# A four-layer graph network on one core: another order of the first loads, and batch norms worked out block by block

## The chip, the core and the metric

The kernel runs on one core of one Trainium2 chip. The metric is the device time of one execution in microseconds (us); a median stands for several executions. A profile is one of these executions, with every instruction's start and length.  Each group of experiments went to one chip, whose number came with the results: 15, 11 and 13.

Engines in the profile: PE is TensorE (PEld its weight loads), DVE is VectorE, ACT is ScalarE, POOL is GpSimd, SP is SyncE; SPq, ACTq and POOLq are their issues of DMA transfers. A line number such as L339 is a line of the kernel named. The change moves lines: L320 of the kernel before is L339 of the changed one (first matmul of layer 1's second product, "the first second-layer matmul" below), L266 is L285 (py), L762 is L775, L834 is L842 to L845.

Names in the profile lines: in layer 0, pt and xt are transposes of x and their copies; pq the query and value products; zs the gathered rows and es the attention scores made of them; adc the row copies of a quad's attention matrix; py its product with the values, yt the copy of that, po the product that follows. In layer 3, ag is the aggregate, ph (from ag) the first half's product and po (from z or zl) the second half's.

## The reference, cut to what matters

x is 128 batches of 128 nodes with 256 features. Four layers follow each other; after each, the input is added and a layer norm taken.

```python
# layer 0: attention over 512 edges
e = einsum(leaky_relu(Xq[:, src] + Xq[:, dst]), a) + log(adj[src, dst] + 1e-8)
attn = segment_softmax(e, src);  Y[src] += attn * Xv[:, dst];  return Y @ W_out.T
# layer 1: h = relu(S @ (x @ W1)); h = relu(S @ (h @ W2)); S @ (h @ W3), with S = adj * adj
# layer 2: three products with the diagonal, upper and lower part of adj, plus a bias
# layer 3: two batch norms, each over all 128 * 128 rows
h = relu(batchnorm(agg @ W1.T + b1, g1, be1))
out = batchnorm(h @ W2.T + b2, g2, be2)
```

Each batch norm needs sums over the whole batch: everything before it must be finished before anything after it starts.

## The kernel before

Batches go in 32 quads of four. Layers 0, 1, 2 and the first half of layer 3 run as one software pipeline, an iteration per quad. `start()` fills this pipeline: it sorts the edges, takes the first quads through attention and loads the weights in between. Then the second half of layer 3 runs over all quads, and an output part normalizes, adds and stores. The parts that matter here:

```python
# start(), cut
    xg1 = load_x(1, "xg", 2)
    ... wo, w1 loaded;  zeros stored to att_dram[0]
    values_in(0, xg0, nc.scalar.copy);  values(0, 0..3)       # TensorE; q stored to DRAM
    ... edges sorted on TensorE;  gather(0) on GpSimd
    nc.scalar.activation(weight, weight, AF.Ln)
    values_in(1, xg1, nc.scalar.copy);  values(1, 0..3)
    ... xg3, w2, xr0 loaded;  zeros stored to att_dram[1]      # 3.5 MB with w1
    for c in range(NE):
        score(0, c)                                            # VectorE, needs gathered rows
    gather(1, ...)
    ... softmax of quad 0;  attention(0);  scatter(0)          # 4 GpSimd scatters, then a 1 MB load
    ... w3, l2w, bias, l3w1 loaded
    gather(2);  score(1, 0..2)
    for j in range(QB):
        by_row(0, j)                                           # ScalarE: row copies of the load
    stage_a(0)                                                 # py, yt, po
    values_in(3, xg3);  values(3, 0..3);  ...
    attention(1);  scatter(1)                                  # before the loop
# hidden(k, c): layer 3's first half, block c
    nc.scalar.copy(s.zt[:, c, :], ph)
    nc.vector.bn_stats(st1[:, c, k, :], ph)
# after the loop: b1, g1, be1, w2t, b2, g2, be2 are loaded through GpSimd, then
    sc1, sh1 = batch_norm(st1, K3, b1, g1, be1, "n1")          # all four blocks at once
    ... second half of layer 3 over all quads, then
    sc2, sh2 = batch_norm(st2, DC, b2, g2, be2, "n2")
# apply(q), the output of a quad: four multiplications on ScalarE, one store by GpSimd
```

## Time and profile before

| | |
|---|---|
| timed executions | 3437.02, 3444.74, 3446.68 us |
| profiled execution | 3427.55 us, span 3425.8 us |
| TensorE busy | 97% of the span |
| first second-layer matmul | 128.65 us |
| one quad in the loop | 93.21 us |
| stop before layer 3's second half | 11.28 us |
| one quad in that half, in the output part | 6.866, 3.06 us |

The page shows the span in 40 slices; each digit is the busy share of a slice in tenths:

```profile
PE   5899999999999999999999999999999999989987
DMA  7512333333323222333333323222333331024447
```

TensorE is full except in the first slices, around slice 36 and at the end. A gain of some microseconds can only come from there. The profiled execution is faster than every timed one, by 9 us or more.

### The profile page before, as it was taken

What the parts mean: (1) busy time and instruction counts of PE and PEld (TensorE: products, weight loads), DVE (VectorE), ACT (ScalarE), POOL (GpSimd) and SP (SyncE); (2) the same over time, 40 slices, a digit from 0 to 9 for tenths busy, and PEclk for the clock granted to TensorE, in tenths of its full rate; (3) what the DMA queues carried; (4) which work ended last, traced back from release to release, by engine and by line L of the source; (5) the groups of instructions that cost most, each with busy time, mean ns of one, the idle gap of its engine ahead of it and who ended that gap; (6) DMA issues with size and microseconds to landing.
All of it is one profiled execution on the core that took longest, in us unless ns stands there. A gap on an engine that the chain in (4) does not pass through costs nothing.

```text
span 3425.8 us, 34423 instructions
## 1 busy us (share of the span) xinstructions
PE 3326.6 (97%) x13328; PEld 2111.0 (62%) x13328; DVE 1715.3 (50%) x3367; ACT 1016.9 (30%) x1751; POOL 641.9 (19%) x535
## 2 busy tenths in 40 slices
PE   5899999999999999999999999999999999989987
PEld 2566666666666666666666666666666666654444
DVE  6545555444554544555445554554555444223358
ACT  2222222222222222222222222222222222225438
POOL 4211222222211111222122221111122220000015
PEclk8899999999999999999999999999999999999999
DMA  7512333333323222333333323222333331024447
GB/s 227 159 46 87 96 99 99 99 87 99 99 80 99 82 74 80 93 99 99 99 87 99 99 81 98 87 77 72 92 99 99 99 93 38 19 88 152 153 156 250
DMA packets 117316, 346.01 MB, mean 101 GB/s; under 512 B 12832, under 2 KB 50080, under 8 KB 108832
## 3 DMA queue, kind: packets, MB, share of 16 engines
q0 software_dynamic: 46032, 152.61, 18.0%
q1 hardware_dynamic: 69344, 189.48, 15.4%
q8 instruction: 106, 1.74, 0.2%
q10 hardware_dynamic: 1776, 1.71, 0.2%
q14 instruction: 58, 0.48, 0.0%
HBM read 257.77 MB, written 85.98 MB: 100 GB/s over the span
## 4 chain that ended last, share of the span: by engine, by line
PE 94%; ACT 2%; DVE 2%; DMA 1%; issue 0%; POOL 0%; ACTq 0%; POOLq 0%; DVEq 0%
PE ph L320 26%; PE p L333 13%; PE po L381 10%; PE po L762 6%; PE ph L421 6%; PE pq L170 6%; PE ph L300 6%; PE po L275 3%; PE pm L310 3%; PE pm L367 3%; PE py L266 2%; PE po L344 2%; PE pm L286 2%; PE pa L406 2%; ACT x3l L833 1%; PE pt L372 1%
## 5 line engine op out<-in xcount | busy, mean ns | idle before, releaser
L320 PE MATMUL ph<-m,w 128*128 128x512 f32 x2048 | 884.2, 592 | 0.0
L320 PEld LDWEIGHTS ph<-m,w 128*128 128x128 f32 x2048 | 389.0, 190 | 476.1 <-issue 474.5
L186 POOL DMA_INDIRECT zs<-qd,src_idx x124 | 147.6, 1191 | 1715.7 <-DMA qd<-qt 1678.5
L333 PE MATMUL p<-w,h 128*128 128x256 f32 x2048 | 450.5, 381 | 0.0
L333 PEld LDWEIGHTS p<-w,h 128*128 128x128 f32 x2048 | 386.6, 190 | 53.0 <-issue 1.0
L381 PE MATMUL po<-l2w,ms 128*128 128x256 f32 x1536 | 347.5, 379 | 1.3 <-DVE ms L373 1.3
L323 ACT ACTIVATE h<-ph 128x512 f32<-128x512 f32 x256 | 152.8, 597 | 585.3 <-PE ph L320 585.2
L381 PEld LDWEIGHTS po<-l2w,ms 128*128 128x128 f32 x1536 | 284.3, 190 | 36.2 <-DVE ms L373 1.6
L170 PE MATMUL pq<-wqv,xt 128*128 128x512 f32 x512 | 232.9, 608 | 7.8 <-DVE xt L158 4.0
L300 PE MATMUL ph<-w,mx 128*128 128x512 f32 x512 | 235.8, 593 | 0.0
L421 PE MATMUL ph<-ag,l3w 128*128 128x512 f32 x512 | 225.4, 593 | 0.8 <-ACT ag L410 0.8
L186 POOL DMA_INDIRECT zs<-qd,dst_idx x124 | 195.1, 1574 | 139.8 <-DMA zs<-qd,src_idx 123.4
L762 PE MATMUL po<-zl,l3w 128*128 128x512 f32 x496 | 213.0, 592 | 0.0
L346 DVE TENSOR_TENSOR xr<-xr,po 128x512 f32<-128x512 f32 x64 | 43.8, 684 | 334.9 <-PE po L344 334.9
L242 POOL DMA_INDIRECT attd<-at,att_idx x128 | 127.5, 996 | 425.9 <-DMA attd<-at,att_idx 285.3
L158 DVE COPY xt<-pt 128x512 f32<-128x512 f32 x58 | 37.4, 686 | 279.9 <-PE pt L156 279.9
L421 PEld LDWEIGHTS ph<-ag,l3w 128*128 128x128 f32 x512 | 96.9, 190 | 122.1 <-issue 112.6
L92 ACT ACTIVATE ln_sd<-ln_mv,eps 128x2 f32<-128x2 f32 x192 | 56.5, 294 | 388.2 <-DVE ln_mv L87 388.2
L170 PEld LDWEIGHTS pq<-wqv,xt 128*128 128x128 f32 x512 | 97.2, 195 | 119.9 <-issue 110.5
L762 PEld LDWEIGHTS po<-zl,l3w 128*128 128x128 f32 x496 | 94.2, 190 | 118.6 <-issue 115.0
L100 DVE TENSOR_SCALAR xr<-xr,ln_mv,ln_rs 128x256 f32<-128x256 f32 x384 | 162.9, 466 | 6.9
L310 PEld LDWEIGHTS pm<-wt_t,h 128*128 128x128 f32 x1024 | 131.8, 191 | 47.7 <-issue 39.9
(201 smaller groups left out, 4112.6 us busy)
## 6 DMA issues: line engine op xcount, KB each, us to landing
ad<-attd SPq DMA_DIRECT2D x32, 1024.0 KB, 4.8
zd<-z SPq DMA_DIRECT2D x31, 1024.0 KB, 7.9
zl<-zd SPq DMA_DIRECT2D x62, 512.0 KB, 4.2
xg<-in_x_dram SPq DMA_DIRECT2D x32, 512.0 KB, 4.3
xr<-in_x_dram SPq DMA_DIRECT2D x32, 512.0 KB, 5.8
x3d<-xr SPq DMA_DIRECT2D x32, 512.0 KB, 2.9
x3l<-x3d SPq DMA_DIRECT2D x32, 512.0 KB, 4.3
out_dram<-x3l POOLq DMA_DIRECT2D x32, 512.0 KB, 4.6
```

The source lines that it names most:

```text
L100: nc.vector.tensor_scalar(r[:, i, :], r[:, i, :], mv[:, i, 0:1], rs[:, i:i + 1], op0=ALU.subtract, op1=ALU.mult)
L170: nc.tensor.matmul(pq, s.xts[i // 2][:, i % 2, c, :], wqv[:, c, :], start=(c == 0), stop=(c == DC - 1))
L186: nc.gpsimd.indirect_dma_start(out=s.z[c], out_offset=None, in_=s.qd, in_offset=bass.IndirectOffsetOnAxis(ap=idx[:, c:c + 1], axis=0), com ...
L242: nc.gpsimd.indirect_dma_start(out=ad, out_offset=bass.IndirectOffsetOnAxis(ap=att_idx[:, c:c + 1], axis=0), in_=s.at[:, c, :], in_offset= ...
L300: nc.tensor.matmul(ph, s.mx[i // 2 * 2][:, i % 2, dc, :], w1_sb[:, dc, :], start=(dc == 0), stop=(dc == DC - 1))
L310: nc.tensor.matmul(pm[:, c, :], s.h1[i][:, c * P:(c + 1) * P], wt_t, start=True, stop=True)
L320: nc.tensor.matmul(ph, w2_sb[:, c, f * P:(f + 1) * P], s.m2[:, c].rearrange("p b n -> p (b n)"), start=(c == 0), stop=(c == K1 - 1))
L323: nc.scalar.activation(h.rearrange("p b n -> p (b n)"), ph, AF.Relu)
L333: nc.tensor.matmul(p3[:, t * D:(t + 1) * D], s.h2[f][:, j + t, :], w3_sb[:, f, :], start=(f == 0), stop=(f == K2 - 1))
L381: nc.tensor.matmul(po[:, i % 2, :], mss[i][:, t, dc, :], l2w[:, t, dc, :], start=(n3 == 0), stop=(n3 == 3 * DC - 1))
L421: nc.tensor.matmul(ph, l3w1[:, dc, c * P:(c + 1) * P], s.ag[:, dc, :], start=(dc == 0), stop=(dc == DC - 1))
L762: nc.tensor.matmul(po, w2t[:, c, o * P:(o + 1) * P], z[c // 2][:, c % 2, :], start=(c == 0), stop=(c == K3 - 1))
```

## The change

Intent: let nothing that is needed late compete with the first quad's attention; have the parameters of layer 3 on the chip before they are needed; let TensorE go on with a block of layer 3 as soon as that block's statistics are known; shorten the end. The core of the diff:

```diff
@@ start(): loads @@
             xg1 = load_x(1, "xg", 2)
+            nc.sync.dma_start(att_dram[0][...], zero)
             nc.sync.dma_start(wo, ...)
-            nc.sync.dma_start(w1_sb, ...)
-            nc.sync.dma_start(att_dram[0][...], zero)
@@ start(): quad 1 straight behind src_row, ahead of the logarithm @@
+            values_in(1, xg1, nc.scalar.copy)
+            for i in range(QB):
+                values(1, i, nc.scalar.copy, nc.scalar)
+            gather(1, [...])
...
             nc.scalar.activation(weight, weight, AF.Ln)
-            values_in(1, xg1, nc.scalar.copy)   # and values(1, ..), gather(1) further below
...
             xg3 = load_x(3, "xg", 2)
-            nc.sync.dma_start(w2_sb, ...)
             quads[0].xr = load_x(0, "xr", 3, wk)
-            nc.sync.dma_start(att_dram[1][...], zero)
...
             scatter(0)
+            nc.sync.dma_start(w1_sb, ...)
+            nc.sync.dma_start(w2_sb, ...)
+            nc.sync.dma_start(att_dram[1][...], zero)
...
+            nc.sync.dma_start(w2t, ...)          # and the six vectors of layer 3
             for j in range(QB):
-                by_row(0, j)
+                by_row(0, j, nc.vector.tensor_copy if j % 2 else None)
             stage_a(0)
-            values_in(3, xg3)
+            values_in(3, xg3, nc.scalar.copy)
...
-            attention(1)
-            scatter(1)
@@ iteration(): in the first one @@
                     second(c, f)
+                    if first_one and f == 0:
+                        attention(b)
+                        scatter(b)
@@ hidden(k, c) @@
+            if k < NQ - 1:
+                nc.scalar.copy(s.zt[:, c, :], ph)
             nc.vector.bn_stats(st1[:, c, k, :], ph)
             if k == NQ - 1:
+                batch_norm(st1, c, bn1, sc1, sh1, c)
+                nc.scalar.activation(s.zt[:, c, :], ph, AF.Relu, bias=sh1[...], scale=sc1[...])
@@ second half of layer 3: last quad first, its matmuls block by block; after the last quad's stats @@
+                    if q == order[-1]:
+                        batch_norm(st2, o, bn2, sc2, sh2, K3 + o)
+                        halves(0, o, outs[0])
+                        spread(o)
                     nc.vector.tensor_copy(ag[:, o, :], po[o])
@@ apply(): the last quad @@
+                    if q == NQ - 1 and i < 2:
+                        nc.vector.tensor_scalar(x3s[q][:, i, :], src_, mvs[q][:, i, 0:1], rs[:, i:i + 1], ...)
+                if q == NQ - 1:
+                    nc.sync.dma_start(o_q[:, :2], x3s[q][:, :2, :])
+                    nc.scalar.dma_start(o_q[:, 2:], x3s[q][:, 2:, :])
```

Some small buffers share space to make room for w2t and the vectors (the zeros take m2's buffer, three adjacency tiles one scratch buffer).

## The prediction

> **What bounds the kernel now.** I read the table by stage first (busy time of each engine in stretches of the span), then the chain that ended last, then TensorE's own timeline. From the table (columns: stretch, busy us and instruction count of each engine, granted TensorE clock, DMA share, GB/s):
>
> ```profile
> 0.00:30.00 30.00, 20.99 (x75) 11.48 (x76) 16.43 (x50) 8.07 (x16) 14.30 (x18) 0.97 0.74 236
> 30.00:60.00 30.00, 14.79 (x61) 9.24 (x61) 18.60 (x20) 4.62 (x11) 11.15 (x9) 0.74 0.96 284
> 60.00:90.00 30.00, 9.36 (x40) 4.77 (x40) 16.95 (x26) 7.37 (x15) 15.03 (x14) 0.71 0.69 184
> ...
> 1000.00:1100.00 100.00, 100.00 (x444) 66.47 (x444) 50.75 (x99) 28.23 (x47) 21.37 (x18) 1.00 0.36 105
> ...
> 3050.00:3080.00 30.00, 19.44 (x81) 13.59 (x80) 14.01 (x33) 4.99 (x10) 5.42 (x8) 0.94 0.52 176
> ```
>
> In the loop TensorE is busy 100 us of 100, so nothing the change does there can pay. It is idle in the first 129 us, around 3075 and near the end. The same places in TensorE's timeline (start, length, operation, in brackets the idle time before it and its releaser):
>
> ```profile
> 55.76 1.02 PE L208 MATMUL pe<-ident,es 128*16 128x128 f32 x4 [15.21 <-DVE es L201]
> ...
> 88.72 3.99 PE L266 MATMUL py<-adc,xv 128*64 128x128 f32 x32 [16.85 <-ACT adc L252]
> ...
> 101.53 9.82 PE L170 MATMUL pq<-wqv,xt 128*128 128x512 f32 x16 [3.98 <-DVE xt L158]
> ```
>
> Two holes of 15.21 and 16.85 us hang on the first quad's attention. What lies behind them, from the chain (start, length, piece):
>
> ```profile
> 41.00 10.51 DMA qd<-qt
> ...
> 67.64 7.89 DMA attd<-at,att_idx
> 75.53 0.27 issue
> 75.81 2.14 DMA attd<-at,att_idx
> ...
> 82.71 4.88 DMA ad<-attd
> ...
> 3076.80 6.06 DMA be<-in_l_be_dram
> 3082.89 221.92 PE po L762 x512
> ```
>
> Quad 1's store takes 10.51 us because 2 MB of w2, 0.5 MB of x and 1 MB of zeros were issued at 37 to 39 us. That holds up quad 1's gather on GpSimd, and the scatter of quad 0's attention stands behind that gather. The last two lines show the batch norm waiting for parameters fetched only after layer 3's first half: TensorE stops for 11.28 us (3071.6 to 3082.9). From 3082.9 to 3304.8 TensorE is full; then it waits 5.38 us for the second batch norm. The output part runs at 3.06 us a quad with ScalarE full (20.00 us of 20 between 3360 and 3380).
>
> **What the Trainium skill says.** "DMA: Bandwidth & Descriptors", section "Issuing engines are not separate DMA queues": transfers of all issuing engines run on the same 16 DMA engines and interleave. The trace agrees: the DMA share is 0.96 between 30 and 60 us, and the store issued by ScalarE is slow because of loads issued by SyncE. "TensorE: Matmul & The Clock Gate", "What's actually happening": after a window of idling the array runs at half clock for about 3.4 us. Here, after the 11.28 us stop, weight loads come 0.86 us apart until 3087.05 and 0.43 us afterwards, so a stop costs about 2 us on top of itself. "ScalarE: Activation LUTs", "What ACT_TABLE_LOAD costs": 1283 ns plus a drain; the trace has 1.28 us. I need this for the moved logarithm.
>
> **Part 1, first loads (all times us; ~ marks my estimates).** w1, w2 and the second zero transfer (3.5 MB) move behind the load of quad 0's attention matrix. Quad 1's values are no longer interrupted: before, ScalarE sat on the logarithm until 27.5 and held xt. Now its copies run after src_row at 23.9, TensorE starts at ~24.5, 16 records of 0.43 end at ~31.4, and the store is issued at ~31.8 instead of 41.0. The price: the logarithm comes after these copies. Table load ~32.2 to 33.5, then 0.2, then four VectorE operations of 0.2, so VectorE stands idle from 27.4 to ~33.8 and the keep/reset rows (2.13) end at ~36.6. So the first score starts at ~36.6, not 33.23. But before, the third and fourth scores waited 4.72 and 1.84 for gathered rows; now, with four scores of 3.78 back to back and 0.45 of small work, es is ready at ~52.1 rather than 55.7. That is only 3.6 saved, because the wait for data becomes a wait for VectorE.
> The softmax (8.05 from its first scan to the attention values) then ends at ~61.3 instead of 64.87. GpSimd has by then issued quad 1's gather (start ~40, 16 us as before), so the scatter starts at once: four steps of 2.4 end at ~71 to 73, where before the first step alone took 7.89 and the load was issued at 82.71. The load takes ~5, landing at ~77 (before 87.59).
> Then VectorE: half of the row copies move to it, behind three scores of quad 1 which, after the 4.4 of adjacency work from ~64.4, end at ~80. py therefore ends at ~82.7 instead of 92.71: 10.0 saved, not the ~13 that leaving the VectorE queue aside would give. The xt copies of quad 3 on ScalarE no longer wait for the layer norm's last multiplications (~1.0). Putting quad 1's attention behind the first block of layer 1 takes about 1.5 of wait before it and puts 0.8 of transposes behind it (~0.7). Sum **11.7**: the first L320 matmul at ~117 instead of 128.65.
> Will the later weights be late? Behind the load at ~72 stand 6.4 MB, with 4 MB of quad 2's gather. Between 82.7 and 111 the old trace moved about 8 MB beside its gather, 0.28 MB/us; 1 + 6.4 + 4.2 MB need ~41, but w1, w2 and the zeros come first: 4.5 MB plus most of the gather, until ~101. w2 is wanted at ~117, the zeros' buffer (now shared with m2) at ~108. So no wait, with some 7 to spare.
>
> **Part 2, first batch norm.** Removed: the seven late loads. For each of four row blocks there is now a chain on VectorE: stats 0.70, aggregate 0.93, root on ScalarE 0.30 with two handovers, reciprocal, product, shift of ~0.18 each: ~2.53. TensorE delivers a block each 1.72, so VectorE sets the pace: from 3066.5, four chains end at ~3076.6, the last relu at ~3077.3. The matmuls go block by block, the first at 3071.65 without a stop, and the last block's pair ends at ~3079.0. Before, this quad ended at 3304.82 - 31 x 6.866 = 3091.97. Saved **13.0**, of which 11.28 is the stop and the rest the half clock, less ~0.5 of new wait.
>
> **Part 3, second batch norm.** The first half's norm (2.6, then 0.4 spread, 0.67 copy) hides under the second half's 3.43 of matmuls. After the last matmul one chain of 2.6 + 0.4 remains; transposes can start at ~3.3 and the identity matmul, which waits for the shift row, copy (0.4) and GpSimd's add (1.3), at ~6.8, against 8.9 before. The two passes over the old columns and the half clock stay. Saved **~2.9**. The 31 steady quads stay at 3.06: ScalarE has the same work.
>
> **Part 4, the end.** In the last quad two of four multiplications (0.5 each on ScalarE) go to VectorE beside the others: 1.0. The single 512 KB output through GpSimd, issued at 3420.90, ended 4.9 later; two 256 KB halves from SyncE and ScalarE should take ~2.5 (a 512 KB store by SyncE lands in 2.6 to 2.9). Saved **~3.2**.
>
> Sum 11.7 + 13.0 + 2.9 + 3.2 = 30.8. From the median 3444.74: **3414**.
>
> **Rivals.** (a) The delayed logarithm and the VectorE queue eat the first part. For: VectorE loses 6.4 at 27.4 to 33.8 and is in order. If the gather still arrives as late as before (51.71 for the last score), part 1 shrinks to ~6: 3420. (b) The 6.4 MB burst delays the zeros, w2 or the row load. For: the old loads there took 24.8 to 25.7 us to land. Against: the order within the burst. Cost 5 to 10: 3419 to 3424. (c) A larger gain: scatter and load in an emptier DMA system go faster and py ends at ~79; part 1 becomes 15: 3410. (d) Part 2 nearly fails, if VectorE's chains cost 3.5 each rather than 2.53 (four handovers): last relu ~4 later, 3418.
>
> **Range and chances.** The parts err by about 4 (part 1), 1.5, 1 and 1.5; the timed runs of before spread over 9.7 and lie 9 to 19 above the profiled execution (3427.55), which gives the after median another ~6. So 3402 to 3426. Two per cent is 69 us; all TensorE idleness outside the loop that the change touches is below that, so faster 0.02; slower would need 100 us of new waits in a loop whose order is unchanged: 0.01.
>
> **What would show it.** The first L320 matmul at 113 to 123; the two holes of 15.21 and 16.85 shrunk to ~13.5 and ~10, with a new stop of ~3 in front of the second pcol; VectorE idle at 27 to 34; the second-layer matmuls of layer 3 following the first without a gap over 1 us; ~3.3 instead of 5.38 before the output part; a last store of ~2.5. Wrong if the loop between the first L320 and 3060 changes its length by more than 3 us, if TensorE waits for w1, w2 or the zeros near 110, or if the output part leaves 3.06 a quad.

## The result, and the profile after

The changed kernel took 3411.68 us (median of four: 3409.24 to 3413.39); the kernel before, in the same rounds, 3442.18 (3437.02 to 3446.68). The ratio is 0.9911, with a 95% interval of 0.9894 to 0.9929. 30.5 us were saved, 0.9%.

The table by stage of the changed kernel (stretch, busy us and instruction count of PE, PEld, DVE, ACT, POOL, then granted clock, DMA share, GB/s), for two stretches that the prediction shows for the kernel before:

```profile
60.00:90.00 30.00, 13.98 (x74) 9.75 (x73) 20.42 (x40) 5.86 (x11) 15.53 (x14) 0.72 0.73 233
...
3050.00:3080.00 30.00, 26.85 (x101) 17.20 (x100) 16.44 (x43) 9.80 (x18) 0.00 (x0) 1.00 0.49 175
```

TensorE is busy 13.98 us between 60 and 90 where it was 9.36, and 26.85 of 30 around the first batch norm where it was 19.44. Its timeline in the first part (start, length, line, operation, in brackets the idle time before it and what ended that):

```profile
34.95 6.40 PE L583 MATMUL pcol<-ends,w 128*128 128x2 f32 x32 [3.14 <-DVE ends L620]
51.99 1.02 PE L227 MATMUL pe<-ident,es 128*16 128x128 f32 x4 [10.64 <-DVE es L220]
...
78.03 1.12 PE L285 MATMUL py<-adc,xv 128*64 128x128 f32 x8 [9.75 <-ACT adc L271]
80.16 2.83 PE L285 MATMUL py<-adc,xv 128*64 128x128 f32 x24 [1.01 <-DVE adc L271]
...
90.68 8.59 PE L189 MATMUL pq<-wqv,xt 128*128 128x512 f32 x16 [2.94 <-ACT xt L177]
...
115.10 3.70 PE L339 MATMUL ph<-m,w 128*128 128x512 f32 x8 [1.43 <-DVE m L330]
```

The holes of 15.21 and 16.85 us are 10.64 and 9.75 plus 1.01, there is a new stop of 3.14, and the first second-layer matmul comes at 115.10. Nothing waits for w1, w2 or the zeros. Around the first batch norm and before the output part:

```profile
3065.47 7.13 PE L440 MATMUL ph<-ag,l3w 128*128 128x512 f32 x16 [0.23 <-ACT ag L429]
3072.44 3.60 PE L775 MATMUL po<-z,l3w 128*128 128x512 f32 x8
3076.36 1.98 PE L775 MATMUL po<-z,l3w 128*128 128x512 f32 x4 [0.33 <-ACT z L448]
3079.00 1.98 PE L775 MATMUL po<-z,l3w 128*128 128x512 f32 x4 [0.65 <-ACT z L448]
...
3297.63 0.44 PE L799 MATMUL pt<-ident,agg 128*128 128x128 f32 x2 [3.26 <-ACT agg L754]
```

The kernel before had at the same two places:

```profile
3082.89 9.04 PE L762 MATMUL po<-z,l3w 128*128 128x512 f32 x16 [11.28 <-DMA be<-in_l_be_dram]
...
3310.18 1.19 PE L782 MATMUL shift_ps<-wide,ones 128*128 128x256 f32 x2 [5.38 <-DVE wide L779]
```

The stop of 11.28 us is gone, with two small waits left; 5.38 became 3.26. The end, in the timeline of all engines, first of the kernel before, then of the changed one:

```profile
3417.63 0.29 ACT L852 ACTIVATE sd<-mv,eps 128x4 f32<-128x4 f32 x1
...
3420.90 0.75 POOL L834 DMA_DIRECT2D out_dram<-x3l  x1 [1.54 <-ACT x3l L833]
```

```profile
3405.44 0.29 ACT L863 ACTIVATE sd<-mv,eps 128x4 f32<-128x4 f32 x1
...
3406.96 0.39 SPq L842 DMA_DIRECT2D out_dram<-x3l  x1
3407.27 0.40 ACTq L843 DMA_DIRECT2D out_dram<-x3l  x1
```

One thing did not fit. The loop, in which nothing was changed, looked longer: from 93.21 us a quad in the first profile of before to 93.72 us. Over 28 steady quads that is 14.3 us, so the two spans differ by 14.1 us only (3425.8 and 3411.7), while the timed medians differ by 30.5.

### The profile page after: what moved, and what is told of

Its sections match the earlier page's. It is cut to its first block, busy times and chain, and to the rows that moved or that the text cites. A ratio compares the mean times of both kernels' runs of the same rounds, so it can differ in the third digit from the quotient of the medians. Undisturbed runs are those within 1.5% of the kernel's fastest.

```text
span 3411.7 us, 34420 instructions
## 1 busy us (share of the span) xinstructions
PE 3335.0 (98%) x13328; PEld 2109.5 (62%) x13328; DVE 1733.2 (51%) x3380; ACT 1014.8 (30%) x1750; POOL 636.8 (19%) x526
## 5 line engine op out<-in xcount | busy, mean ns | idle before, releaser
L119 DVE TENSOR_SCALAR xr<-xr,ln_mv,ln_rs 128x256 f32<-128x256 f32 x384 | 178.4, 507 | 6.9
```

Of the source, the lines that this page charges most:

```text
L119: nc.vector.tensor_scalar(r[:, i, :], r[:, i, :], mv[:, i, 0:1], rs[:, i:i + 1], op0=ALU.subtract, op1=ALU.mult)
```

## The experiments

For each profile I read the same marks: **pe**, the transposes after the first quad's scores (es is ready just before); **adc**, the first row copy; **py end**; **block**, the first second-layer matmul; the loop's period; **root**, the first root of the output part, counted from the start of the last matmul of layer 3's second half; **end**, from the last root to the end of the span.

| kernel (chip) | pe | adc | py end | block | period | root | end |
|---|---|---|---|---|---|---|---|
| before, first profile | 55.76 | 87.62 | 92.71 | 128.65 | 93.21 | 12.47 | 8.13 |
| before again (15) | 54.42 | 88.14 | 93.23 | 129.71 | 93.70 | 12.21 | 8.14 |
| part 1 alone (15) | 52.05 | 78.33 | 83.16 | 115.13 | 93.70 | 12.30 | 8.13 |
| parts 2 to 4 alone (15) | 55.76 | 86.53 | 91.62 | 127.66 | 93.72 | 9.28 | 6.24 |
| early logarithm (15) | 52.51 | 79.70 | 84.49 | 117.32 | 93.72 | 10.23 | 6.25 |
| weights only (11) | 52.24 | 79.38 | 84.48 | 120.69 | 93.21 | 12.21 | 8.14 |
| order only (11) | 55.87 | 84.12 | 88.92 | 121.53 | 93.21 | 9.28 | 6.23 |
| loads late (11) | 48.93 | 75.97 | 80.76 | 113.18 | 93.21 | 10.23 | 6.24 |
| one store (11) | 52.14 | 77.05 | 83.16 | 116.97 | 93.21 | 9.28 | 6.31 |
| changed, first profile | 51.99 | 76.90 | 82.99 | 115.10 | 93.72 | 10.23 | 6.24 |
| changed again (13) | 52.79 | 77.63 | 83.78 | 116.11 | 93.71 | 10.23 | 6.23 |
| combined (13) | 48.83 | 75.89 | 80.69 | 114.12 | 93.71 | 9.91 | 6.24 |
| attention old (13) | 52.54 | 77.32 | 83.54 | 117.51 | 93.71 | 10.89 | 6.24 |
| copies on ScalarE (13) | 51.86 | 77.70 | 82.82 | 114.83 | 93.71 | 10.23 | 6.24 |

### The kernel before again, and the changed kernel again: whose is the longer loop?

No edit in either. Expected of before:

> The kernel before, unchanged, profiled a second time. In the first profile its loop took 93.21 us per quad and the execution 3427.55, while its timed runs lie at 3437 to 3447; the changed kernel's loop took 93.72 per quad, 14.3 us more over 28 quads. Theory S (the 0.51 us is a property of an execution, not of the kernel): this profile shows 93.7 per quad with a short TensorE wait for the second yt copy, if its time is 3437 or more, and 93.2 if its time is about 3428; first second-layer matmul at 128.7, end of the output part as before. Theory C (the change itself lengthens the loop): 93.21 per quad again in every profile of this kernel, and a time near 3428 or a difference in some other stage.

Expected of the changed kernel:

> The changed kernel, unchanged, a second time. On the chip where four kernels of mine ran first, every profile had a loop of 93.7 us per quad; on the next chip all four had 93.21. If the loop's length is a property of the chip, this kernel shows 93.2 with a time near 3398 on a chip where the kernel before takes some 3429, or 93.7 with a time near 3412 where it takes some 3442, and the ratio is 0.991 within its interval either way. If the change itself lengthened the loop, this kernel shows 93.7 on every chip. Stages otherwise as in its first profile: first second-layer matmul at 115 to 117, end 6.2 after the last root.

Measured: the kernel before took 3442.86 us on chip 15 (ratio to itself 0.9997, interval 0.9984 to 1.0011), with a period of 93.70. The changed kernel took 3414.73 on chip 13, where before took 3446.59 (0.9913, 0.9896 to 0.9929), with 93.71. All four kernels on chip 15 and all four on chip 13 have 93.70 to 93.72; all four on chip 11 have 93.21, and there the kernel before takes 3429.29. So the period is not the change's: the unchanged kernel has it too. My theory had named a single execution; it held for whole groups of runs. Each of the three groups had its own chip and its own time, so the runs can't tell a chip from a session; "chip" below stands for both. The place is the same in both kernels. Here it is in TensorE's timeline, first the kernel before in its first profile:

```profile
1095.08 3.72 PE L275 MATMUL po<-wo,yt 128*128 128x256 f32 x16
```

and the same kernel on chip 15:

```profile
1103.35 1.99 PE L275 MATMUL po<-wo,yt 128*128 128x256 f32 x8
1105.55 1.99 PE L275 MATMUL po<-wo,yt 128*128 128x256 f32 x8 [0.21 <-DVE yt L269]
```

The second eight matmuls wait for VectorE's copy of yt. In VectorE's timeline, in the same order:

```profile
1095.20 0.69 DVE L269 COPY yt<-py 128x512 f32<-128x512 f32 x1 [0.59 <-PE py L266]
```

```profile
1104.81 0.69 DVE L269 COPY yt<-py 128x512 f32<-128x512 f32 x1 [1.93 <-PE py L266]
```

The copy starts 2.02 us after the first py matmul in the first profile (1093.18 to 1095.20) and 3.36 us after it on chip 15 (1101.45 to 1104.81). The copy itself takes 0.69 in both. Why it starts later is not settled: TensorE's semaphore record just before it comes late too (1104.78, against 1095.17), and VectorE's layer-norm multiplications take 508 ns in the mean there, against 467.

So the first profile of before most likely came from a chip of the quick kind, its timed runs (3437 and more) from one of the other: 28 times 0.49 is 13.7 us, and 3427.55 plus 13.7 is 3441.3, within their range. Compared on chips of one kind, the spans are 3444.1 (before again) and 3411.7 or 3412.6 (changed): 32.4 or 31.5 apart. By stages, before again minus the changed kernel: block 14.61, from there to layer 3's first half of the last quad 2.42, from there to the last matmul of the second half 12.49, root 1.98, the roots of the output part -0.99, end 1.90; the sum is 32.41.

### Part 1 alone, and parts 2 to 4 alone: do the parts add?

```diff
# part 1 alone: before, with the change's edits of start() and iteration(), without w2t and the vectors
# parts 2 to 4 alone: before, with the change's batch_norm(), hidden(), second half and apply(), and
             nc.sync.dma_start(l3w1, ...)
+            nc.sync.dma_start(w2t, ...)      # and the six vectors
```

> Part 1 alone: the order of the first loads, quad 1's values and gather, the row copies. The parts-add theory: first L-second-layer matmul of the loop at 115 to 117 instead of 128.7, everything after the loop as before (stop of 11.3 before layer 3's second half), time about 12 to 13 below the kernel before. Rival (the loop pays it back): loop period 93.7 in this kernel and 93.2 in the kernel before, so that the time falls by 0 to 2 only.

> Parts 2 to 4 alone: both batch norms by row block with early parameters, and the split end; the first loads as before, with the parameters behind layer 3's first weights. Parts-add theory: first second-layer matmul of the loop at 128.7 as before, no stop before layer 3's second half (12 saved), 2.2 saved before the output part, 1.9 at the end: about 16 below the kernel before. If the changed loop period comes from the constants' new places in the on-chip memory, it is 93.7 here and 93.2 in the part-1 kernel.

Measured on chip 15, where before took 3441.22: part 1 alone 3429.07 (0.9962, 0.9948 to 0.9975), parts 2 to 4 alone 3422.35 (0.9938, 0.9925 to 0.9952). The medians fall by 12.15 and 18.87, together 31.0, as against 30.5 for the whole change: they add, and neither is paid back. Parts 2 to 4 gave more than the 16 I expected. In their profile the second batch norm gains 2.93 (12.21 to 9.28), not the 2.2 seen in the changed kernel; and 5.1 of the distance to the profile of before again lies in stages that this kernel does not change (block 2.05, loop 3.05). The profile of before again was the slowest execution of its five, and part of the reason is TensorE's clock (see the experiment with attention at its old place).

### Weights only, and order only: which half of part 1 does it?

```diff
# weights only: the kernel before
-            ... w1, w2, zeros at their old places
             scatter(0)
+            nc.sync.dma_start(w1_sb, ...);  nc.sync.dma_start(w2_sb, ...)
+            nc.sync.dma_start(att_dram[1][...], zero)
# order only: the changed kernel with the same three moved back (and the first zeros behind w1 again)
```

> The kernel before with w1, w2 and the second zero transfer behind the load of quad 0's attention matrix (zeros in the buffer of m2, as in the change), and nothing else: quad 1's values, gather and the row copies stay where they were. The first second-layer matmul comes at 128.7 to 129.7 in the kernel before and at 115.1 with all of part 1. Traffic theory (the 3.5 MB make quad 1's store and gather slow, and the scatter stands behind that gather): 118 to 121, that is two thirds or more of the gain. Order theory (the gain comes from doing quad 1's values earlier): 124 or later.

> The changed kernel with w1, w2 and the second zero transfer back at their old places; quad 1's early values and gather, the moved logarithm and the shared row copies stay. Traffic theory: the first second-layer matmul falls back to 123 or later, with the scores waiting for gathered rows between 37 and 60. Order theory: 118 or earlier. If the two parts add, its loss and that of the weights-only kernel sum to 13.5 to 14.6; if they overlap, the sum differs.

Measured on chip 11: weights only 3419.56 (0.9973, 0.9956 to 0.9990), block at 120.69; order only 3403.94 (0.9926, 0.9909 to 0.9942), block at 121.53. Kernels with the old first loads have their block at 128.65, 129.71 and 127.66 (mean 128.67), those with the whole of part 1, not counting edits to it, at 115.10, 116.11, 116.97 and 115.13 (mean 115.83). So weights alone gain 8.0, order alone 7.1, both 12.8: they overlap by 2.3. The traffic theory held for the weights-only kernel and missed the other (it wanted 123 or later); the order theory missed both. The marks tell them apart. The scores' end comes from the weights alone: pe is at 52.24 without the reordering and at 55.87 with it but with the old weights. What the order gives lies later, half of it before py end (from pe to there 33.05, where the three profiles with the old first loads have 35.86 to 38.81) and half after it (from py end to block 32.61 instead of 36.21).

### Early logarithm, then also late loads: what sets the scores?

```diff
# early logarithm: the changed kernel
             values_in(1, xg1, nc.scalar.copy)
-            values(1, 0..3);  gather(1)
             ...
             nc.scalar.activation(weight, weight, AF.Ln)
+            values(1, 0..3);  gather(1)
# loads late: also
-            xg3 = load_x(3, "xg", 2)
-            quads[0].xr = load_x(0, "xr", 3, wk)
             ...
             scatter(0)
+            quads[0].xr = load_x(0, "xr", 3, wk)
+            xg3 = load_x(3, "xg", 2)
```

> The changed kernel with the logarithm put on ScalarE between quad 1's input copies and its value copies. In the changed kernel VectorE stands idle 8.27 us until 34.14 for it. My account: the logarithm ends at about 26.6, the scores start at about 29.6, then wait for gathered rows again (the last one issued at 40.2), so es is ready at 47 to 48 instead of 52.0 and the first second-layer matmul comes at 110 to 111 instead of 115.1: 4 to 5 us faster than the changed kernel. Rival (the gather, not VectorE, sets es, or the adjacency work and quad 1's scores set the row copies): es moves by less than 2 us or the matmul by less than 2.

> The kernel with the early logarithm, and now also the loads of quad 3's x and quad 0's residual x (1 MB) behind the load of quad 0's attention matrix. The early logarithm alone moved es from 52.0 to 52.5 only: the scores then waited for gathered rows 5.02, 1.10 and 0.82 us. If that wait is a matter of DMA traffic between 24 and 45 us (1 of some 7 MB less), es is ready at 47.5 to 50 and the first second-layer matmul comes at 110 to 113. Rival (the gather's own descriptors and its order behind quad 1's store set it, whatever else is in flight): es at 51.5 or later and the matmul at 115 to 117.

Measured: the early logarithm alone took 3415.72 on chip 15 (0.9917, 0.9904 to 0.9931), no gain, block at 117.32: my account (es at 47 to 48) failed, and its rival held. With the late loads it took 3395.23 on chip 11 (0.9898, 0.9882 to 0.9915), block at 113.18 (0.2 later than I had it), pe at 48.93; the one-store kernel below, the changed one but for its end, took 3397.34 on the same chip, with block at 116.97. In the changed kernel VectorE's timeline has the wait for the logarithm and then all scores without a gap:

```profile
34.14 0.16 DVE L617 SCALAR_TENSOR_TENSOR ends<-small,small 128x4 f32<-128x4 f32 x1 [8.27 <-ACT small L616]
```

With the early logarithm the same scores wait for the gathered rows:

```profile
35.27 1.23 DVE L215 SCALAR_TENSOR_TENSOR zs<-zs 128x1024 f32<-128x1024 f32 x1 [5.02 <-DMA zs<-qd,dst_idx]
...
40.11 1.22 DVE L215 SCALAR_TENSOR_TENSOR zs<-zs 128x1024 f32<-128x1024 f32 x1 [1.10 <-DMA zs<-qd,dst_idx]
...
48.45 1.23 DVE L215 SCALAR_TENSOR_TENSOR zs<-zs 128x1024 f32<-128x1024 f32 x1 [0.82 <-DMA zs<-qd,dst_idx]
```

and with 1 MB of x out of their way they wait less:

```profile
31.56 1.23 DVE L215 SCALAR_TENSOR_TENSOR zs<-zs 128x1024 f32<-128x1024 f32 x1 [1.51 <-DMA zs<-qd,dst_idx]
...
41.23 1.23 DVE L215 SCALAR_TENSOR_TENSOR zs<-zs 128x1024 f32<-128x1024 f32 x1 [1.55 <-DMA zs<-qd,dst_idx]
```

Two limits stood at the same place: VectorE's delay and the arrival of the rows. Taking one away gave nothing; taking both gave 3 us at pe. Of these, 1.9 and 2.9 us are left at the block, against the two profiles of the changed kernel: the second scatter waits 4.05 us for the first to land (2.32 in the changed kernel), with quad 1's gather and quad 2's store in flight.

### One store at the end

```diff
-                    nc.sync.dma_start(o_q[:, :2], x3s[q][:, :2, :])
-                    nc.scalar.dma_start(o_q[:, 2:], x3s[q][:, 2:, :])
+                    nc.sync.dma_start(o_q, x3s[q])
```

> The changed kernel with the last 512 KB stored in one piece by SyncE after all four multiplications, in place of two halves by SyncE and ScalarE. In the changed kernel the span ends 6.24 us after the last root on ScalarE, in the kernel before (one piece by GpSimd) 8.14. I predicted 2.5 us for a store of 256 KB and saw 4.4 from its issue. If a store's cost here is mostly a fixed delay, one piece ends 6.2 to 6.7 after the root; if it is bytes over bandwidth, 7.0 or more.

Measured: 3397.34 on chip 11 (0.9902, 0.9886 to 0.9919); the end takes 6.31 us, as against 6.24 with two halves. Splitting gives 0.07. By the times of the last packets, the single store lands 2.94 us after its issue; the ScalarE half of the changed kernel 3.02 (3407.27 to 3410.29); the store of the kernel before, through GpSimd, 3.00 (3420.90 to 3423.90). All three last the same. What differs is the issue, 1.83 us after the last root in the changed kernel and 3.27 in the kernel before (1.44 sooner), and the closing of the program after the last packet, 1.40 and 1.86 us (0.46 sooner).

### Attention at its old place, and the row copies on ScalarE

```diff
# attention old: the changed kernel
-                    if first_one and f == 0:
-                        attention(b);  scatter(b)
             ... end of start():
+            attention(1);  scatter(1)
# copies on ScalarE: the changed kernel
-                by_row(0, j, nc.vector.tensor_copy if j % 2 else None)
+                by_row(0, j)
```

> The changed kernel with quad 1's attention and scatter back at the end of the first loads, before the first second-layer matmul. I predicted 0.7 for this move: 1.5 of wait less, 0.8 of transposes pushed behind the first block. Expected: first second-layer matmul 1.5 to 2 later than the changed kernel of this call relative to the end of the py matmuls (32.1 us there), the first loop iteration about 0.8 shorter, so 0.7 to 1.2 in all. Rival: the earlier gain of 3.8 after py (before 35.9, changed 32.1) is mostly this move, and it goes to 35 or more.

> The changed kernel with all four row copies of quad 0 on ScalarE again. In the changed kernel the py matmuls end 6.09 us after the first row copy starts, with a stop of 1.01 for VectorE, which is busy with quad 1's scores until 79.53; in the weights-only kernel, with all copies on ScalarE, 5.10 after. If sharing is worth nothing when the load lands before the scores end, py ends about 5.1 after the first copy here, that is about 1 us sooner. Rival (sharing halves the copies' time): 6.1 or later.

Measured on chip 13 (before 3446.59, changed 3414.73): attention old 3416.23 (0.9910, 0.9892 to 0.9928). From py end to block it takes 33.97 instead of 32.33, so 1.64 more, as expected. But the first loop iteration was not shorter. After its stop of 2.21 us TensorE's clock was halved for a while, which the kernel before shows in one profile and not in the other. The table by stage, some four microseconds from the block on, for the kernel before on chip 15 and in its first profile, and for attention old:

```profile
129.70:133.70 4.00, 4.00 (x6) 1.85 (x6) 3.78 (x5) 0.00 (x0) 1.76 (x1) 0.50 0.01 2
```

```profile
128.65:132.60 3.95, 3.95 (x11) 1.81 (x10) 3.74 (x5) 0.22 (x1) 1.76 (x1) 1.00 0.01 2
```

```profile
117.50:121.50 4.00, 4.00 (x8) 1.69 (x7) 3.78 (x5) 0.00 (x0) 1.75 (x1) 0.64 0.01 2
```

The third number from the end, the granted clock, is 0.50, 1.00 and 0.64 after the same stop. From the block to quad 1's py it takes 30.84 us in the first, 28.10 in the second and 29.80 in attention old. This is not the chip: parts 2 to 4 alone, on chip 15 too, and weights only have the same stop, a clock of 1.00 and 28.10. With attention behind the first block the stop is 1.43, and it took 28.89 or 28.90 in all nine profiles that have it there (0.8 of it for the moved transposes). So the old place cost 1.7 or 2.7 us more in two profiles of five, and the new one in none of nine, which I had not seen.

Why the same stop halves the clock or does not can be read from the clock records in the packed traces: in all fourteen, the clock changes only at whole multiples of 3.41 us from the first record. A stop counts by how it falls into these windows.

Copies on ScalarE: 3410.51 (0.9899, 0.9882 to 0.9915), all four runs (3409.17 to 3412.90) below the four of the changed kernel (3414.35 to 3415.09).

```profile
78.83 3.99 PE L285 MATMUL py<-adc,xv 128*64 128x128 f32 x32 [10.82 <-ACT adc L271]
```

py goes through without the stop of 1.01, and ends 5.12 us after the first row copy instead of 6.15. Sharing the copies with VectorE costs 1 us here, because VectorE is still at quad 1's scores when the load lands. It isn't a loss everywhere: in the five kernels where the load lands later or the scores end sooner (part 1 alone, early logarithm, order only, loads late, combined), py ends 4.79 to 4.83 after the first row copy, 0.3 sooner than with all copies on ScalarE (5.12 here, 5.10 in weights only).

### Combined

```diff
# the loads-late kernel, and in the second half of layer 3
                         spread(o)
-                    nc.vector.tensor_copy(ag[:, o, :], po[o])
+                    else:
+                        nc.vector.tensor_copy(ag[:, o, :], po[o])
+                if q == order[-1]:
+                    for o in range(DC):
+                        nc.vector.tensor_copy(ag[:, o, :], po[o])
```

> The kernel with the early logarithm and the late loads of x, and in the last quad before the second batch norm the copies of both output blocks behind both chains of the norm, so that VectorE does the second chain 0.68 us earlier. Expected: first second-layer matmul at 111 to 114 (113.2 there); from the last matmul of layer 3's second half to the first root 8.6 us if TensorE's clock is not halved after its stop (9.28 in three kernels with it full, 10.23 in three with it at half); time 2 to 5 below the changed kernel of the same call. Rival: the half clock comes anyway and the stage stays at 9.5 or more.

Measured: 3411.00 on chip 13 (0.9900, 0.9884 to 0.9917), 3.7 below the changed kernel's 3414.73 of the same call by the medians, and each of its four runs (3409.67 to 3413.88) below each of the changed kernel's; the intervals of the ratios overlap. The changed kernel's own two sets of four are 3.0 apart and do not overlap either, so neither this 3.7 nor the 4.2 of the copies on ScalarE is well shown; and that edit of one line (3410.51) did as well as this one. Block at 114.12, as expected. The root is at 9.91: the rival was right. TensorE's stop is 2.94 instead of 3.26, and its clock is halved all the same. How much that costs is seen by comparing the changed kernel with the one-store kernel, which is the same there but for its last store; the table by stage from the first identity matmul on:

```profile
3300.40:3305.00 4.60, 4.60 (x15) 3.46 (x16) 2.47 (x9) 1.28 (x3) 2.35 (x2) 0.50 0.00 0
```

```profile
3289.90:3294.50 4.60, 4.60 (x28) 3.33 (x29) 3.36 (x13) 1.70 (x4) 2.38 (x2) 1.00 0.00 0
```

In the same 4.60 us TensorE does 15 matmuls at a clock of 0.50 and 28 at 1.00, after stops of 3.26 and 3.25. The roots come at 10.23 and 9.28. In the windows of 3.41 us, the changed kernel's stop lies mostly in one, with 1.14 us of TensorE work left in it, and the clock is 0.50 in the next; the one-store kernel's is split over two, with 2.02 and 1.46 left, and the clock stays:

```profile
3295.36:3298.77 3.41, 1.14 (x8) 1.09 (x9) 3.17 (x9) 1.13 (x3) 0.00 (x0) 1.00 0.38 139
```

```profile
3281.79:3285.20 3.41, 2.02 (x6) 0.58 (x4) 3.22 (x9) 0.87 (x2) 0.00 (x0) 1.00 0.66 187
3285.20:3288.61 3.41, 1.46 (x11) 1.42 (x12) 3.14 (x10) 1.45 (x4) 0.05 (x1) 1.00 0.31 123
```

## Why the prediction was right or wrong

The time was right: 3414 predicted, 3411.68 measured, and a gain of 30.8 predicted against 30.5 (I had subtracted from the median of three runs, 3444.74; that of four is 3442.18). The sum came out better than its terms, and that is luck. The four parts measured make 28.6: one term was 1.1 too low, three together 3.3 too high. Most of the rest stood in no term: against before again, 2.42 gained between the block and layer 3's first half of the last quad (1.95 of it before quad 1's py, where before again runs at half clock after its stop of 2.21), and 0.99 lost in the output part.

**Part 1: 11.7 predicted, 12.8 measured** (means of the block). Up to py the working held: es at 52.1 (52.0), py end 82.7 (83.0 and 83.8). Two of its reasons were wrong, though. "The price" of the delayed logarithm is none: with the early logarithm es comes no sooner, since the rows arrive no sooner. My "the wait for data becomes a wait for VectorE" was a tie of two limits, which only taking away both shows. And "half of the row copies move to it" is a loss of 1.0, hidden in my sum. The mis-sized term is what follows py. I counted 1.0 for the xt copies and 0.7 for the attention, 1.7 in all; measured are 35.94 before and 32.11 after, 3.8. The attention's move is 1.64 of it at the block (0.8 comes back in the loop), the wait for xt shrank by 1.0 (3.98 to 2.94), and the values of quad 3 went through in 8.59 instead of 9.82, the clock being halved for 3.41 of them and not for 6.83. This last 1.2 can't be counted on: in the one-store and the combined kernel, with the same code at this place, the half clock lasted 6.83, the same values took 10.20 and 10.16, and py end to block 33.81 and 33.43.

**Part 2: 13.0 predicted, 11.9 measured** (239.73 less 227.79 from the last quad's first half to the last matmul of the second half, first profiles; 12.5 against before again). The stop of 11.28 went as said. The step that was too small is the chain: "~2.53" is 2.64 (one statistics start to the next), mostly because an aggregate takes 1.02, not 0.93. Four of them and the last relu end TensorE's block 15.35 us after the first half's start, where I had 14.5.

**Part 3: 2.9 predicted, 2.0 measured against a kernel before on the same kind of chip.** The working was right for a full clock: three kernels with it have 9.28, 2.93 below 12.21. The changed kernel, both times, fell into the half clock after its stop of 3.26. I had written that "the half clock stay[s]" and yet did not carry it through the identity matmuls.

**Part 4: 3.2 predicted, 1.9 measured.** The 1.0 for the multiplications was sound, and together with a shorter way from the last multiplication to the issue it is 1.44. The failed step is the store: "ended 4.9 later" took the closing of the program for part of the store. The Trainium skill, "DMA: Bandwidth & Descriptors", section "Anatomy of one DMA — SWDGE (gpsimd) path", gives a fit of 2.0 us plus the bytes at 436 GB/s for a transfer issued by GpSimd. For 512 KB that is an estimate of 3.2; this trace has 3.00. Had I used it, I would have seen that 1.9 of the 4.9 were something else, and that halves cannot take much off a cost that is mostly fixed.

**The rivals.** (a) did not happen: the gather came sooner than before. (b) did not happen: TensorE waits for no weight. (c) was right about the direction of part 1 and wrong about the place. (d) was a tenth of a microsecond per chain, not one.

**The test for being wrong.** I wrote "Wrong if the loop ... changes its length by more than 3 us". Between the first profiles it changed by 14.5. By my own rule I was wrong; the runs clear the change of it, because the same change of period appears in the unchanged kernel from chip to chip. The mistake was in the base: I set a timeline from one chip under a time from another. It did no harm only because both kernels were timed in the same rounds. One sign failed quietly: the first hole was to shrink to about 13.5, and it shrank to 10.64.

Open: what delays VectorE's copy on chips 13 and 15; and why the output part, steady at 3.05 a quad, has three to five stops of about a microsecond or more whose places differ from program to program (98.6 to 102.0 from first root to last, 0.99 of it against the changed kernel). Of the profiles with the new second batch norm, six of the seven at half clock have one more stop, of 1.8 us, behind the second root, and none of the three at full clock has it; whether the clock brings it is not shown.

## What to carry to other kernels

Before comparing two traces stage by stage, compare a stage that the change cannot touch; if that differs, profile the old kernel again on the same chip before explaining anything. When a wait seems to move from data to an engine, look for a tie: removing either limit alone shows nothing, and the second one is often a load that nobody needs yet. Read a store's cost from its own packets, not from the end of the program.

## What the Trainium skill lacked or had wrong

- "TensorE: Matmul & The Clock Gate", section "What's actually happening": its table puts the cold clock after at least one idle window of about 3.4 us. Here shorter stops were enough: the granted clock was 0.50 and 0.64 in the four microseconds after a stop of 2.21, and 0.50 after stops of 2.94 and 3.26. It was 1.00 after stops of 2.21 and 3.25 in other profiles. So a window need not be wholly idle: one with TensorE busy for 1.14 of 3.41 us was followed by the half clock. The page says that the window is free-running, and the traces agree: all changes of the clock lie on a grid of 3.41 us. How much work keeps the clock up is not settled here.
- No page that I read has that the same loop can run at two steady speeds: 93.21 us per quad in the four kernels of one chip and 93.70 to 93.72 in the eight of two others, for kernels with and without the change (one group of runs on each chip).
- No page that I read has the time from the last packet's landing to the last instruction of the program: 1.40 and 1.50 us with the last store issued by ScalarE or SyncE, 1.86 with it issued by GpSimd.
